# Layer norm of a graph attention block: variance, power and shift for two tiles in one instruction

## The chip, the cores and the metric

The kernel runs on one core of a Trainium2 chip. The metric is the time of one execution on the device in microseconds; lower is better. TensorE is called PE in the profile (its weight loads PEld), VectorE DVE, ScalarE ACT, GpSimd POOL and SyncE SP.

## The reference

The input `x` has 16 graphs of 1024 nodes with 512 features; `adj` is one 1024 x 1024 matrix of zeros and ones for all of them. The layer is multi-head attention over the neighbours of each node (8 heads of 64), an output projection, a residual and a layer norm without learned scale:

```python
q = (x @ Wq + bq).reshape(b, n, H, HD)
k = (x @ Wk + bk).reshape(b, n, H, HD)
v = (x @ Wv + bv).reshape(b, n, H, HD)
scores = jnp.einsum('bqhd,bkhd->bhqk', q, k) / jnp.sqrt(jnp.float32(HD))
scores = scores + (1.0 - adj)[None, None, :, :] * -1000000000.0
attn = jax.nn.softmax(scores, axis=-1)
out = jnp.einsum('bhqk,bkhd->bqhd', attn, v).reshape(b, n, d) @ Wo + bo
y = x + out
return (y - mean(y)) / jnp.sqrt(var(y) + 1e-5)
```

Each node has few neighbours, most of them 1 to 8, a few up to 80 in the kernel's tables.

## The kernel before

Nodes are sorted by their number of neighbours and put into tiles of 128 rows. For a tile, POOL gathers one neighbour's key and value rows per block (tile `kvg`, L1292); VectorE multiplies keys with queries (L1313) and sums per head (L1317), ACT takes the exponentials (L1328) and mostly also weighs the values (L1341), VectorE adds the blocks up (L1357) and divides by the sum of weights (L1387, tile `o`).

One Python loop writes the instructions of all engines in order. It counts block steps, `n` from -39 on; 530 steps are blocks. In each step it issues the exponentials of block n + 3, the products of block n + 4, gathers 8 blocks ahead, the sums, and then what earlier steps have planned: `later(k, fn)` puts `fn` into step n + k, in the middle of the step (list `plan`), and `later_last(k, fn)` puts it at the end of that step, behind ACT's weighting (list `rest`). Every engine works through its own instructions in this order and waits only for data and buffers.

Between these, a step gives PE a number of units, by a credit per step: those of `fronts`, which project x to queries, keys and values of the batches to come (L799 `pq`, L956), and those of `finish`, which multiply a finished tile by Wo (L799 `po`). The list `fronts` lasts until some 45 steps before the last block; the profile's last 165 us or so are that last stretch. There the tiles that had been spilled to memory come back (tile `oTs`).

The layer norm of a tile is written out by `complete` (L1097), one step behind its last matmul. VectorE adds the projected tile to the residual `y` and takes the row sums with it (L1112, L1113; `st[:, 0]`). One step later ACT squares the deviations and sums them (`spread`, L1120; `st[:, 2]`). `variance` (L1123, VectorE) scales that and adds epsilon; `power` (L1126, POOL) takes the power -1/2 (`st[:, 3]`); `shift` (L1129, VectorE) makes minus the mean times that (`st[:, 4]`); `norm_out` (L1134, ACT) applies both to `y`; `store` (L1148, POOL) scatters the rows to the output. VectorE's three are on one column of 128 rows each.

A tile is "single" while `fronts` isn't empty, if it has fewer than 128 rows, and at the very end. A single tile in front of the last stretch has its variance at step +3, its power at +4, its shift at +6 and its normalisation at the end of +7, its store at +9. In the last stretch, tiles of 128 rows go in pairs: the two share a statistics tile of two times five columns, the first waits in `half` for the second, each takes its own variance and its own shift, and POOL takes both powers in one instruction (L1174).

A tile `y` is loaded ahead of its `finish` (`load_y`, L1035 from SP or L1038 from POOL), into one of six buffers, while fewer than five are held; `del Y[b, t]` in `store` gives it back. The `finish` of a tile begins two steps behind its load at the earliest.

Of the kernel before, what the change touches and what calls it, by code (L numbers as in the profile page):

```python
# [14 lines left out]
OP = mybir.AluOpType  # L15
# [3 lines left out]
EPS = 1e-5  # L19
# [55 lines left out]
P = 128  # L75
# [103 lines left out]
def kernel(  # L179
# [36 lines left out]
    nc = tc.nc  # L216
    B, N, D = x.shape
# [37 lines left out]
    with ExitStack() as main:  # L255
# [192 lines left out]
        def later(k, fn):  # L448
            plan.setdefault(now[0] + k, []).append(fn)

        def later_last(k, fn):
            rest.setdefault(now[0] + k, []).append(fn)
# [554 lines left out]
        loaded, half, wide = {}, [], []  # L1007
# [7 lines left out]
        def rows_of(b, t):  # L1015

            if t == LONE_TILE or t == 0 and merged(b):
                n, col, base = (2 * SPARED, NT + 2, b - 1) if t else (P, NT + 1, b - 1)
            elif t == MORE_TILE:
                n, col, base = (LONE - SPARED) * (B - PAIRED_FROM), NT + 3, 0  # L1020
            else:
                n, col, base = P, NT if t == ONE_KEY and b >= PAIRED_FROM else t, b
            return n, asked_row[0:n, col:col + 1], base * N * D
# [19 lines left out]
        def load_lone(b):  # L1043


            Y[b, "mean"] = work.tile([P, D], F32, tag="y", name=f"means_{b}", bufs=Y_BUFS)
            for i in range(2):
                nc.sync.dma_start(
                    Y[b, "mean"][SPARED * i:SPARED * (i + 1), :], mean_rows[b - 1 + i:b + i, :].to_broadcast([SPARED, D])
                )  # L1050
            load_y(b, LONE_TILE)
            later(4, lambda: complete(b, LONE_TILE, Y.pop((b, "mean")), True))
# [15 lines left out]
        def finish(b, t):  # L1068


            mean_row = t == ONE_KEY and b >= PAIRED_FROM
            plain = bool(fronts) or mean_row
            biased = not plain and now[0] < total and number(b, t) in (*SPILL, -1)

            if not plain and not biased and (b, t) != closes[total - 1]:
                nc.vector.tensor_tensor(Y[b, t], Y[b, t], bo_bc, op=OP.add)

            def out(p):
                OT.pop((b, t))
                if mean_row:  # L1080
                    keep_mean(b, p)
                if not fronts and total - 4 < now[0] < total:
                    later(total - now[0], lambda: complete(b, t, p, plain))
                else:
                    complete(b, t, p, plain)

            units = product(f"po_{b}_{t}", lambda c: OT[b, t][:, ts(c, P)], W["o"], out)
            if biased:
                def bias():
                    nc.tensor.matmul(  # L1090
                        PS[f"po_{b}_{t}"], three.to_broadcast([P, P]), bo_3, start=False, stop=False
                    )

                units.insert(2, (BIAS, bias, None))
            return units

        def complete(b, t, p, plain):  # L1097
            n, rows, offset = rows_of(b, t)
            y, p = Y[b, t][0:n, :], p[0:n, :]
            ending = not fronts and now[0] >= total - 1  # L1100
            single = fronts or ending or n < P
            if single:
                st = small.tile([P, 5], F32, name="stats", bufs=6)[0:n, :]
            else:

                second = bool(half)
                if not second:
                    half.append([small.tile([P, 2, 5], F32, name="stats_2", bufs=5)])
                st2 = half[0][0]
                st = st2[:, int(second), :]  # L1110
            if plain:
                nc.vector.tensor_tensor(y, p, y, op=OP.add)  # L1112
            nc.vector.scalar_tensor_tensor(  # L1113
                y, bo_bc[0:n, :] if plain else p, 1.0, y, op0=OP.mult, op1=OP.add, accum_out=st[:, 0:1]
            )

            def spread():

                sq = work.tile([P, D], F32, tag="ysq", name=f"ysq_{b}_{t}", bufs=1)
                nc.scalar.activation(sq[0:n, :], y, AF.Square, bias=st[:, 0:1], scale=-float(D), accum_out=st[:, 2:3])  # L1120

            def variance():
                nc.vector.tensor_scalar(st[:, 2:3], st[:, 2:3], 1.0 / D ** 3, EPS, op0=OP.mult, op1=OP.add)  # L1123

            def power():
                nc.gpsimd.tensor_tensor(st[:, 3:4], st[:, 2:3], neg_half[0:n, :], op=OP.pow)  # L1126

            def shift():
                nc.vector.scalar_tensor_tensor(  # L1129
                    st[:, 4:5], st[:, 0:1], -1.0 / D, st[:, 3:4], op0=OP.mult, op1=OP.mult  # L1130
                )

            def norm_out():
                nc.scalar.activation(y, y, AF.Identity, bias=st[:, 4:5], scale=st[:, 3:4])  # L1134
                if not fronts and now[0] >= total:
                    later_last(1, store)
                else:
                    later(2, store)

            def centre():  # L1140
                nc.vector.tensor_scalar(st[:, 4:5], st[:, 0:1], 1.0 / D, None, op0=OP.mult)

            def last_norm_out():
                nc.vector.tensor_scalar(y, y, st[:, 4:5], st[:, 3:4], op0=OP.subtract, op1=OP.mult)
                store()

            def store():
                nc.gpsimd.indirect_dma_start(  # L1148
                    out=out_rows[b, t], out_offset=bass.IndirectOffsetOnAxis(ap=rows, axis=0),
                    in_=y, in_offset=None, element_offset=offset,  # L1150
                )
                del Y[b, t]

            later_last(0 if ending else 1, spread)
            if ending and (b, t) == closes[total - 1]:
                for step in (centre, variance, power, last_norm_out):
                    later(1, step)
            elif ending:
                later(1, variance)
                later(1, power)  # L1160
                later_last(1, shift)
                later_last(1, norm_out)
            elif single:
                late = 1 if fronts else 0
                later(2 + late, variance)
                later(3 + late, power)
                later(4 + 2 * late, shift)
                later_last(5 + 2 * late, norm_out)
            elif second:
                later(3, variance)  # L1170
                mate_shift, mate_norm_out = half.pop()[1]

                def powers():
                    nc.gpsimd.tensor_tensor(  # L1174
                        st2[:, :, 3:4], st2[:, :, 2:3], neg_half[:, :, None].to_broadcast([P, 2, 1]), op=OP.pow
                    )

                def shifts():
                    mate_shift()
                    shift()  # L1180

                later(4, powers)
                shift_at = 6 if fronts else min(6, max(5, total - now[0]))
                later(shift_at, shifts)
                later_last(shift_at, mate_norm_out)
                later_last(7 if shift_at == 6 else 5, norm_out)
            else:
                later(3, variance)
                mine = half[0]
                mine.append((shift, norm_out))  # L1190

                def alone():
                    if half and half[0] is mine:
                        half.pop()
                        power()
                        later(2, shift)
                        later_last(3, norm_out)

                later(6, alone)

# [281 lines left out]
        done, coming, spilled, gathered, fronts, guarded = [], [], [], [0], [], []  # L1484
# [31 lines left out]
        with tc.manual_schedule():  # L1516
# [20 lines left out]
            n = -LEAD_IN  # L1537
# [120 lines left out]
```

## Time and profile before

| | |
|---|---|
| runs | 1845.62, 1847.8, 1847.21 us |
| median | 1847.21 us |
| span of the profiled execution (its whole time is not given) | 1840.4 us |
| mean granted clock of PE over the span | 0.996 |
| DMA, mean | 303 GB/s |

The profile is of one execution. Its page lists the busy time of each engine, the span in 40 slices, and the costliest groups of instructions; further views give the waits, the instructions in order of time and the busy time by stretch. Some rows of the page's slices and groups, for orientation:

```profile
PE   7999999999999999999999999999999999999997
...
DVE  6889889999989999999999999999999999997986
ACT  3637869989889898999889988989799999987886
POOL 1367766766565776767757666677666767665786
PEclk9999999999999999999999999999999999999998
...
L1341 ACT ACTIVATE pv<-kvg,pv 128x64 f32<-128x64 f32 x3600 | 907.5, 341 | 0.0
L1292 POOL DMA_INDIRECT kvg<-kv_pair,place_row x462 | 526.7, 1140 | 307.4 <-ACT pv L1341 99.6
...
L1134 ACT ACTIVATE y<-y,stats 128x512 f32<-128x512 f32 (+1 forms) x128 | 102.7, 806 | 17.0 <-DVE stats L1129 17.0
```

A digit is the busy share of one slice of 46 us in tenths. In a group's row stand the line, engine, operation, output and inputs with their shapes and the count; then the busy time, the mean of one in ns, and the idle time of the engine just before, with what ended most of it.

### The profile page before, as it was taken

What the parts mean: (1) busy time and instruction counts of PE and PEld (TensorE: products, weight loads), DVE (VectorE), ACT (ScalarE), POOL (GpSimd) and SP (SyncE); (2) the same over time, 40 slices, a digit from 0 to 9 for tenths busy, and PEclk for the clock granted to TensorE, in tenths of its full rate; (3) what the DMA queues carried; (4) which work ended last, traced back from release to release, by engine and by line L of the source; (5) the groups of instructions that cost most, each with busy time, mean ns of one, the idle gap of its engine ahead of it and who ended that gap; (6) DMA issues with size and microseconds to landing.
All of it is one profiled execution on the core that took longest, in us unless ns stands there. A gap on an engine that the chain in (4) does not pass through costs nothing.

```text
span 1840.4 us, 25352 instructions
## 1 busy us (share of the span) xinstructions
PE 1798.2 (98%) x5140; PEld 876.2 (48%) x5140; DVE 1693.7 (92%) x3473; ACT 1563.2 (85%) x6183; POOL 1215.3 (66%) x1142
## 2 busy tenths in 40 slices
PE   7999999999999999999999999999999999999997
PEld 3444454554444454444444445444544444444443
DVE  6889889999989999999999999999999999997986
ACT  3637869989889898999889988989799999987886
POOL 1367766766565776767757666677666767665786
PEclk9999999999999999999999999999999999999998
DMA  7358787989889899999988998999989999889995
GB/s 287 106 190 253 256 325 237 346 301 327 308 280 314 295 336 319 344 316 308 347 316 310 346 335 276 343 321 322 339 315 325 314 355 326 306 324 325 338 319 191
DMA packets 198791, 558.54 MB, mean 303 GB/s; under 512 B 33450, under 2 KB 33470, under 8 KB 198626
## 3 DMA queue, kind: packets, MB, share of 16 engines
q0 software_dynamic: 112640, 370.50, 59.3%
q1 hardware_dynamic: 82910, 180.52, 26.2%
q10 hardware_dynamic: 3076, 5.82, 0.9%
q14 instruction: 122, 1.00, 0.2%
q8 instruction: 43, 0.70, 0.2%
HBM read 420.30 MB, written 157.45 MB: 314 GB/s over the span
## 4 chain that ended last, share of the span: by engine, by line
PE 69%; DVE 10%; ACT 9%; DMA 4%; issue 3%; POOL 1%; SPq 0%; POOLq 0%; DVEq 0%; ACTq 0%
PE po L799 17%; PE pq L799 15%; PE pp L956 12%; PE z L956 9%; PE x L956 9%; ACT pv L1341 5%; DVE qk L1313 2%; PE poT L1401 2%; PE pxT L757 2%; PE sum L1367 2%; DVE s L1317 2%; PE sum L1366 2%; DVE pv L1357 1%; ACT sq_k L809 1%; DMA kvg<-kv_pair,place_row 1%
## 5 line engine op out<-in xcount | busy, mean ns | idle before, releaser
L1341 ACT ACTIVATE pv<-kvg,pv 128x64 f32<-128x64 f32 x3600 | 907.5, 341 | 0.0
L1292 POOL DMA_INDIRECT kvg<-kv_pair,place_row x462 | 526.7, 1140 | 307.4 <-ACT pv L1341 99.6
L799 PE MATMUL pq<-wq,xT 128*128 128x512 f32 x792 | 367.8, 596 | 0.0
L1317 DVE TENSOR_REDUCE s<-qk 128x8 f32<-128x512 f32 x530 | 360.7, 681 | 6.8
L799 PE MATMUL po<-wo,oT 128*128 128x512 f32 x792 | 359.3, 594 | 0.7 <-ACT oT L1405 0.7
L1313 DVE TENSOR_TENSOR qk<-qt,kvg 128x512 f32<-128x512 f32 x434 | 297.2, 685 | 1.1 <-DMA kvg<-kv_rows,key_row 0.6
L956 PE MATMUL x<-b,xT 128*128 128x512 f32 x504 | 237.3, 593 | 0.5 <-ACT e L969 0.4
L956 PE MATMUL pp<-t,s 128*128 128x512 f32 x504 | 237.0, 593 | 0.0
L1357 DVE TENSOR_TENSOR pv<-pv,pv 128x520 f32<-128x520 f32 x329 | 228.3, 694 | 4.3 <-ACT pv L1341 4.2
L799 PEld LDWEIGHTS po<-wo,oT 128*128 128x128 f32 x792 | 149.1, 191 | 170.0 <-issue 160.2
L799 PEld LDWEIGHTS pq<-wq,xT 128*128 128x128 f32 x792 | 148.4, 192 | 161.9 <-issue 149.9
L1010 POOL DMA_INDIRECT x<-in_x_dram,asked_row x120 | 133.0, 1108 | 77.8 <-issue 21.3
L1148 POOL DMA_INDIRECT out_dram<-y,asked_row x129 | 146.9, 1139 | 39.1 <-issue 21.2
L1328 ACT ACTIVATE pv<-s,absent 128x8 f32<-128x8 f32 x434 | 127.0, 294 | 44.0 <-DVE s L1317 40.8
L809 ACT ACTIVATE sq_k<-kv 128x128 bf16<-128x128 f32 x512 | 150.8, 301 | 6.4 <-DVE kv L979 3.4
L956 PEld LDWEIGHTS pp<-t,s 128*128 128x128 f32 x504 | 94.7, 191 | 108.1 <-issue 99.4
L956 PEld LDWEIGHTS x<-b,xT 128*128 128x128 f32 x504 | 94.2, 191 | 107.4 <-issue 99.0
L956 PE MATMUL z<-b,s 128*128 128x512 f32 x252 | 119.2, 596 | 7.0 <-DVE kv L984 7.0
L1246 POOL DMA_INDIRECT qg<-q_rows,query_row x96 | 104.4, 1088 | 28.4 <-issue 26.9
L956 PE MATMUL z<-t,s 128*128 128x512 f32 x252 | 118.6, 593 | 0.0
L956 PE MATMUL pp<-t,xT 128*128 128x512 f32 x252 | 118.5, 593 | 0.0
L1134 ACT ACTIVATE y<-y,stats 128x512 f32<-128x512 f32 (+1 forms) x128 | 102.7, 806 | 17.0 <-DVE stats L1129 17.0
(279 smaller groups left out, 2713.0 us busy)
## 6 DMA issues: line engine op xcount, KB each, us to landing
kv_pair<-kv SPq DMA_DIRECT2D x98, 512.0 KB
q_rows<-q SPq DMA_DIRECT2D x106, 256.0 KB
qt<-q_rows SPq DMA_DIRECT2D x98, 256.0 KB
residual<-x SPq DMA_DIRECT2D x83, 256.0 KB
y<-residual SPq DMA_DIRECT2D x83, 256.0 KB
kv_rows<-kv SPq DMA_DIRECT2D x15, 512.0 KB
kvg<-kv_pair,place_row POOLq DMA_INDIRECT x462, 6.9
kv_pair<-kv SPq DMA_DIRECT2D x28, 256.0 KB
```

The costliest lines, as they stand in the source:

```text
L799: nc.tensor.matmul(p, lhs(c), w[:, c, :], start=(c == 0), stop=(c == NPAIR - 1))
L809: nc.scalar.activation(sq, s[:, ts(h, P)], AF.Square, scale=scale, accum_out=sums[:, h:h + 1])
L956: nc.tensor.matmul(R[bank], l[:, ts(c, P)], right[:, c, :], start=(first and c == 0), stop=(c == 1), skip_group_check=True,)
L1010: nc.gpsimd.indirect_dma_start(out=y, out_offset=None, in_=x_rows, in_offset=bass.IndirectOffsetOnAxis(ap=asked_row[:, t:t + 1], axis=0), ...
L1148: nc.gpsimd.indirect_dma_start(out=out_rows[b, t], out_offset=bass.IndirectOffsetOnAxis(ap=rows, axis=0), in_=y, in_offset=None, element_o ...
L1246: nc.gpsimd.indirect_dma_start(out=q, out_offset=None, in_=q_rows[b % ROWS], in_offset=bass.IndirectOffsetOnAxis(ap=rows, axis=0))
L1292: nc.gpsimd.indirect_dma_start(out=KG[n], out_offset=None, in_=rows, in_offset=bass.IndirectOffsetOnAxis(ap=(place_row if b else key_row)[ ...
L1313: nc.vector.tensor_tensor(QK[n], q, KG[n][:, 0:D], op=OP.mult)
L1317: nc.vector.tensor_reduce(S[n], QK.pop(n).rearrange("p (h d) -> p h d", d=HD), axis=AX.X, op=OP.add)
L1328: nc.scalar.activation(PV[n][:, D:], S.pop(n), AF.Exp, bias=bias)
L1341: nc.scalar.activation(pv[:, ts(h, HD)], v[:, ds(D + h * HD, HD)], AF.Copy, scale=pv[:, D + h:D + h + 1])
L1357: nc.vector.tensor_tensor(PV[b, t], PV[b, t], pv, op=OP.add)
```

## The change

A tile of 128 rows is now paired in the whole kernel, not only in the last stretch; single are tiles of fewer rows and those at the very end. Of a pair, the variance and the shift are one VectorE instruction over two columns each, as the power on POOL already was. The steps are counted from the second tile: variances +3, powers +4, shifts +6 (fewer near the end, as before), the first tile's normalisation at the end of the step of the shifts, the second's one step later. A first tile that gets no mate within 9 steps (5 in the last stretch, where it was 6) goes on alone: its variance in that step, power +1, shift +3, normalisation at the end of +4.

```diff
-            single = fronts or ending or n < P
+            single = ending or n < P
...
             elif second:
-                later(3, variance)
-                mate_shift, mate_norm_out = half.pop()[1]
+                mate_norm_out = half.pop()[1]
+
+                def variances():
+                    nc.vector.tensor_scalar(
+                        st2[:, :, 2:3], st2[:, :, 2:3], 1.0 / D ** 3, EPS, op0=OP.mult, op1=OP.add
+                    )
 
                 def powers():
                     nc.gpsimd.tensor_tensor(
...
                 def shifts():
-                    mate_shift()
-                    shift()
-
+                    nc.vector.scalar_tensor_tensor(
+                        st2[:, :, 4:5], st2[:, :, 0:1], -1.0 / D, st2[:, :, 3:4], op0=OP.mult, op1=OP.mult
+                    )
+
+                later(3, variances)
                 later(4, powers)
                 shift_at = 6 if fronts else min(6, max(5, total - now[0]))
                 later(shift_at, shifts)
                 later_last(shift_at, mate_norm_out)
                 later_last(7 if shift_at == 6 else 5, norm_out)
             else:
-                later(3, variance)
                 mine = half[0]
-                mine.append((shift, norm_out))
+                mine.append(norm_out)
 
                 def alone():
                     if half and half[0] is mine:
                         half.pop()
-                        power()
-                        later(2, shift)
-                        later_last(3, norm_out)
-
-                later(6, alone)
+                        variance()
+                        later(1, power)
+                        later(3, shift)
+                        later_last(4, norm_out)
+
+                later(9 if fronts else 5, alone)
```

## The prediction

> **What bounds the kernel now.** I read the page first (shares of busy time), then the busy time by stretch, then what TensorE waits for.
>
> ```profile
> span 1840.4 us, 25352 instructions
> ...
> PE 1798.2 (98%) x5140; PEld 876.2 (48%) x5140; DVE 1693.7 (92%) x3473; ACT 1563.2 (85%) x6183; POOL 1215.3 (66%) x1142
> ...
> 200.00:1650.00 1450.00, 1436.76 (x4156) 706.20 (x4155) 1378.11 (x2700) 1301.16 (x5300) 982.09 (x903) 1.00 0.91 317
> 1650.00:1790.00 140.00, 138.95 (x381) 65.49 (x380) 119.89 (x299) 111.76 (x385) 101.64 (x93) 1.00 0.92 327
> 1790.00:1841.00 51.00, 36.66 (x93) 16.78 (x92) 32.20 (x100) 35.13 (x103) 31.39 (x33) 0.88 0.55 202
> ```
>
> The last three rows give, for a stretch, its length and the busy time of PE, PEld, DVE, ACT and POOL, then the granted clock. From 200 to 1650 us, where pairing is new, PE is idle 1450 - 1436.8 = 13.2 us; in the next 140 us, 1.1 us. A busy PE need not be one at its peak, so I look at how fast the matmuls follow one another.
>
> ```profile
> 1000.02 1.88 PE L956 MATMUL pp<-t,s 128*128 128x512 f32 x4
> ...
> 1001.74 3.60 PE L799 MATMUL pq<-wq,xT 128*128 128x512 f32 x8
> ...
> 1005.17 1.88 PE L956 MATMUL x<-b,xT 128*128 128x512 f32 x4
> ```
>
> Four matmuls start in 1.72 us and eight in 3.43: one per 0.43 us, while the records last 0.59, so each runs into the next and nothing stands between them. The granted clock is 1.00. PE is therefore the bound from 200 to 1790 us, and a change that gives PE nothing less to do can win at most its 14.3 us of idle time there and something at the end.
>
> ```profile
> PE z L956 <- DVE kv L984: 5.9, 4, 3.0
> ...
> PE pm L867 <- DVE vsum L863: 3.1, 3, 1.9
> ...
> PE poT L1401 <- DVE o L1387: 2.6, 1, 2.6
> ...
> PE pq L799 <- DVE y L1112: 0.8, 1, 0.8
> ```
>
> These are PE's waits from 200 to 1650 us (total, times, longest): 12.4 us, all on VectorE. VectorE is the neighbour that matters, and the change takes instructions off it.
>
> **The change: VectorE.** A tile's layer norm has a variance (L1123), a power on POOL (L1126, or L1174 for two), a shift (L1129) and the normalisation on ACT (L1134).
>
> ```profile
> L1123 DVE TENSOR_SCALAR stats<-stats x129: 131/145/155, 195.7 to 1832.2; 128x1 f32<-128x1 f32 x121, 112x1 f32<-112x1 f32 x8
> ...
> L1129 DVE SCALAR_TENSOR_TENSOR stats<-stats x128: 137/151/202, 209.0 to 1830.4; 128x1 f32<-128x1 f32 x120, 112x1 f32<-112x1 f32 x8
> ...
> L1126 POOL TENSOR_TENSOR stats<-stats,neg_half x97: 543/585/1852, 205.6 to 1832.9; 128x1 f32<-128x1 f32 x89, 112x1 f32<-112x1 f32 x8
> L1174 POOL TENSOR_TENSOR stats<-stats,neg_half x16: 717/794/1761, 1699.5 to 1815.7; 128x2 f32<-128x2 f32 x16
> ...
> 1714.72 0.15 DVE L1378 TENSOR_TENSOR rden<-sum,pv 128x8 f32<-128x8 f32 x1
> 1714.79 0.68 DVE L1379 TENSOR_TENSOR o<-sum,pv 128x512 f32<-128x512 f32 x1
> ...
> 1718.91 0.22 DVE L1129 SCALAR_TENSOR_TENSOR stats<-stats 128x1 f32<-128x1 f32 x2
> 1719.05 0.15 DVE L1123 TENSOR_SCALAR stats<-stats 128x1 f32<-128x1 f32 x1
> 1719.11 0.69 DVE L1113 SCALAR_TENSOR_TENSOR y<-po,y 128x512 f32<-128x512 f32 x1
> ```
>
> A small record lasts 145 or 151 ns, but what it costs VectorE is when the next one starts: two shifts take 0.14 us (1718.91 to 1719.05), a variance 0.06. I take 67 and 62 ns. An instruction over two columns isn't in the trace on VectorE; one over eight (L1378) lets the next start after 0.07 us, one over one column after 0.06 to 0.07, so two columns cost no more than one.
>
> How many pairs? The order of VectorE's records tells the block step of each sum L1113: count the products L1313 ahead of it. While x is still being projected, full tiles come 2 to 12 steps apart. A first tile waits up to 9 steps for its mate. Going through the steps gives 38 pairs (from steps 11 and 15 to steps 475 and 480) and 8 tiles that stay alone; then the 16 pairs of L1174 as now. Removed on VectorE: 38 x (62 + 67) ns = 4.9 us in the first stretch, 16 x 129 ns = 2.1 us in the last.
>
> Little of that reaches PE, because VectorE catches up whenever it has to wait itself. The two longest waits of PE for z show it:
>
> ```profile
> 544.95 0.43 DVE L783 TENSOR_TENSOR s<-xT 128x256 f32<-128x256 f32 x1 [2.96 <-PE z L956]
> ...
> 549.82 1.98 PE L956 MATMUL z<-b,s 128*128 128x512 f32 x4 [2.38 <-DVE kv L984]
> ...
> 1063.61 0.43 DVE L783 TENSOR_TENSOR s<-xT 128x256 f32<-128x256 f32 x1 [0.35 <-ACT xT L761]
> ...
> 1065.88 1.98 PE L956 MATMUL z<-b,s 128*128 128x512 f32 x4 [3.01 <-DVE kv L984]
> ```
>
> In brackets stands the idle time before. VectorE was idle itself until 544.95 and 1063.61, and between that and the end of PE's wait it runs no variance and no shift. These 5.4 us stay. In the unbroken runs before the other waits I count 18 small instructions in all; with 0.4 of them gone, 18 x 0.4 x 0.065 = 0.5 us. Bounds: 0, and the whole 4.9.
>
> In the last stretch the power is paired already. There the one long wait of PE is
>
> ```profile
> 1808.33 1.02 PE L1401 MATMUL poT<-ident,o 128*128 128x128 f32 x4 [3.09 <-DVE stats L1123]
> ```
>
> The transpose needs o (L1387), which VectorE makes after a run of 15.6 us without a gap, with 8 small instructions in it; four go: 4 x 0.065 = 0.3 us. Bounds: 0 and 2.1.
>
> **The change: POOL.** 38 times two powers become one: 38 x (2 x 585 - 794) ns = 14 us. POOL also issues the gathers behind the power, but VectorE's wait for a gathered block is small:
>
> ```profile
> DVE qk L1313 <- DMA kvg<-kv_pair,place_row: 1.3, 2, 0.8
> ```
>
> I take 0, at best -1.3 us.
>
> **The change: ACT, the wait that is added.** A single tile has its shift at step +6 and its normalisation at the end of step +7. In a pair the first tile's normalisation stands at the end of the very step of the shift. Behind it in ACT's queue are the next exponentials, the weighting and the copies of e, xT and oT that PE waits for. In the last stretch this is so now:
>
> ```profile
> ACT y L1134 <- DVE stats L1129: 10.0, 6, 3.5
> ...
> ACT y L1134 <- DVE stats L1129: 7.0, 6, 1.5
> ...
> ACT e L969 <- PE x L956: 58.2, 29, 5.1
> ...
> PE po L799 <- ACT oT L1405: 0.3, 1, 0.3
> ```
>
> The first row is of 1650 to 1790 us, the second of the end: 17.0 us over 16 pairs. Nothing of the kind is listed from 200 to 1650 us, where all tiles are single. For each of the 38 steps I compared when the mate's shift ends with when ACT is through its weighting of that step. At the median ACT comes 1.5 us after the shift and would not wait; in 8 of 38 it comes earlier, by 8.3 us in total. The worst place:
>
> ```profile
> 268.32 0.71 ACT L1120 ACTIVATE ysq<-y,stats 128x512 f32<-128x512 f32 x1
> ...
> 270.20 0.15 DVE L1129 SCALAR_TENSOR_TENSOR stats<-stats 128x1 f32<-128x1 f32 x1
> ...
> 270.32 0.30 ACT L1328 ACTIVATE pv<-s,absent 128x8 f32<-128x8 f32 x1 [1.20 <-DVE s L1317]
> ```
>
> Here ACT would be held from about 268.4 to 270.4. Since ACT has slack towards PE (it waits 58.2 us for PE's x alone, PE for ACT 0.3 us, the last two rows of the fence before), I take +0.2 us; bounds 0 and 8.3.
>
> **The change: tiles held longer.** A first tile is stored up to 7 steps later. At most four loaded tiles are let stand beside a new one. By the steps this delays a load once, near step 485, where the projections end, by one step. If PE misses a product there it loses 4 x 0.43 = 1.7 us; the products behind find free steps, so I take 0. A load into a buffer not yet stored costs SP, not PE, as far as the trace shows (before 1650 us and after it):
>
> ```profile
> SPq L1035 <- DMA out_dram<-y,asked_row: 1.4, 1, 1.4
> ...
> SPq L1035 <- DMA out_dram<-y,asked_row: 36.1, 7, 15.5
> ```
>
> **The sum.** -0.5 - 0.3 + 0 + 0.2 + 0 = -0.6 us: a span of 1839.8 us. What lies around that execution's span is not given; the three runs shown are 5.2 to 7.4 us above it, their median, 1847.21, by 6.8. With 6.8 around it I forecast 1846.6.
>
> **Rivals.**
>
> *VectorE is the bound after all.* Then the 4.9 + 2.1 = 7.0 us come off whole: 1847.2 - 7.0 = 1840.2. For it: 1378 of 1450 us busy, and every wait of PE above is for VectorE. Against it: the matmuls without gaps and only 13.2 us of idle PE, 5.4 of them in places without a small instruction. A milder form, in which shorter runs on VectorE dissolve some waits of 2 to 3 us each, ends at about the same time. 0.22. The Trainium skill, "Perfetto Trace Analysis", section "Identifying the Most-Contended Engine", says that a matmul's busy share is no measure of the room left and that the weight loads' share is one. By that rule the 48% of PEld would leave PE half free and make VectorE the engine to relieve, as in this rival; the pitch of 0.43 us speaks against it here.
>
> *ACT waits for the shift.* The mechanism of the last section but two: the first tile's normalisation stops ACT's queue until VectorE reaches the shift, at the 8 places counted, and it goes through to PE in full: 1847.2 + 8.3 = 1855.5. It decides as soon as ACT runs ahead of VectorE in the step of the shift, as it does in the last stretch. Against it: ACT comes 1.5 us late at the median. 0.13.
>
> *It does not pair.* If mates mostly missed each other, nothing would change: 1847.2. The gaps of 2 to 12 steps speak against it. 0.03. *The delayed load costs a tile's turn at the end.* There the sums of successive tiles come 3.7 us apart:
>
> ```profile
> 1822.98 0.69 DVE L1113 SCALAR_TENSOR_TENSOR y<-po,y 128x512 f32<-128x512 f32 x1
> ...
> 1826.73 0.68 DVE L1113 SCALAR_TENSOR_TENSOR y<-po,y 128x512 f32<-128x512 f32 x1
> ```
>
> This would give 1847.2 - 0.8 + 3.7 + 1.7 = 1851.8. 0.05.
>
> By a page the saving of the first part would be larger: the Trainium skill, "VectorE: DVE Perf Modes", section "The TRN2 errata — SBUF-src ops pay a fixed extra latency per instruction", states a measured fixed term of about 150 cycles, 156 ns at its 0.96 GHz, so 108 instructions would save 17 us of VectorE. The pitch of 62 to 67 ns in this trace is less than half of that, and the sum above goes by the pitch.
>
> **How the numbers follow.** Forecast 0.57, the rivals 0.22, 0.13, 0.03, 0.05. A measurement of this kernel can tell about 0.2%, 3.7 us, from no change. The forecast's own range is 1843.5 to 1850: PE's waits of 2 to 3 us fall differently whenever instructions shift. The range goes down to the first rival and stops short of the second: 1839.5 to 1852. Faster: 0.22 + 0.03 of the forecast's low end = 0.25. Slower: 0.13 + 0.05 = 0.18. Within: 0.57.
>
> **What would show it.** Right: about 54 rows of two columns on each of L1123's successor, L1174 and the shift; PE's idle time from 200 to 1650 us still 10 to 16 us, its waits still on kv, vsum and o; a wait of ACT's L1134 for the shift now listed in that stretch, under 10 us. Wrong: idle time of PE there under 7 us (first rival), or over 20 with waits on ACT's copies (second); a hole in PE near 1680 us or a longer end (the last one).

## The result, and the profile after

| | before | after |
|---|---|---|
| median | 1847.21 us (1844.56 to 1849.67, 5 runs) | 1857.11 us (1852.9 to 1857.58, 5 runs) |
| span of the profiled execution | 1840.4 us | 1853.3 us |
| mean granted clock | 0.996 | 0.992 |

The ratio is 1.0045, with a 95% interval of 1.0033 to 1.0057: the change makes the kernel about 8 us slower by the ratio, 9.9 us by these medians. The forecast was 1846.6 us and the range ended at 1852. The two spans lie 12.9 us apart, more than the medians: a span is 1.8 us below the time of its own execution (in one of the runs below 1868.5 us beside 1870.28), so the profiled execution of the kernel before took about 1842 us, less than any of its five runs, and some 3 of the 12.9 us are the choice of execution.

The page of the changed kernel: busy time, share and instructions of each engine.

```profile
PE 1801.7 (97%) x5140; PEld 875.8 (47%) x5140; DVE 1687.6 (91%) x3365; ACT 1563.6 (84%) x6183; POOL 1200.4 (65%) x1104
```

VectorE has 3473 - 3365 = 108 instructions fewer and POOL 1142 - 1104 = 38 fewer, which is what the change should remove. Its groups by line show the pairs: name, count, then shortest, median and longest in ns, and the times of the first and the last.

```profile
L1173 DVE TENSOR_SCALAR stats<-stats x54: 152/161/418, 213.5 to 1825.3; 128x2 f32<-128x2 f32 x54
L1178 POOL TENSOR_TENSOR stats<-stats,neg_half x54: 714/750/1761, 220.8 to 1826.1; 128x2 f32<-128x2 f32 x54
L1183 DVE SCALAR_TENSOR_TENSOR stats<-stats x54: 141/153/197, 228.2 to 1828.9; 128x2 f32<-128x2 f32 x54
```

So it pairs, and VectorE and POOL are relieved. Busy time by stretch, changed kernel (length, then PE, PEld, DVE, ACT, POOL, granted clock):

```profile
200.00:1650.00 1450.00, 1437.25 (x4154) 704.88 (x4153) 1372.62 (x2625) 1300.45 (x5298) 965.72 (x865) 1.00 0.90 317
1650.00:1790.00 140.00, 135.75 (x370) 63.85 (x369) 115.17 (x266) 108.76 (x373) 95.78 (x88) 0.99 0.90 321
```

Where the pairing is new, PE is idle for 1450 - 1437.3 = 12.7 us, against 13.2; in the next 140 us it is idle for 4.2 us, against 1.1. The waits from 200 to 1650 us (total, times, longest) are the old ones and one more of ACT:

```profile
ACT y L1134 <- DVE stats L1183: 8.0, 7, 2.0
...
PE z L956 <- DVE kv L984: 6.5, 5, 2.9
...
PE pm L867 <- DVE vsum L863: 2.6, 3, 2.0
PE poT L1407 <- DVE o L1393: 2.5, 1, 2.5
```

The loss is all behind 1650 us, where the power had been paired before. PE in order of time, changed kernel (start, duration, line and tiles; in brackets the idle time before and its end):

```profile
1706.09 3.41 PE L799 MATMUL po<-wo,oTs 128*128 128x512 f32 x4 [3.34 <-DMA oTs<-spill]
...
1816.00 1.12 PE L1407 MATMUL poT<-ident,o 128*128 128x128 f32 x4 [8.93 <-DVE o L1393]
1816.90 3.62 PE L799 MATMUL po<-wo,oTs 128*128 128x512 f32 x4
1820.32 0.63 PE L1090 MATMUL po<-bo,three 128*128 128x512 bf16 x1
```

PE waits 3.3 us at 1706, for a spilled sum that is loaded late, and at 1816 for `o` 8.93 us, where it had waited 3.09. From that transpose to the end of the span it is 1853.3 - 1816.0 = 37.3 us; before, 1840.4 - 1808.3 = 32.1. Behind the transpose stand six output products in place of five. One of them, which starts at 1823.79, takes 3.65 us until the next starts.

What makes `o` late? VectorE sits idle twice shortly before, each time for a power on POOL. The changed kernel:

```profile
1797.71 0.16 DVE L1183 SCALAR_TENSOR_TENSOR stats<-stats 128x2 f32<-128x2 f32 x1 [3.02 <-POOL stats L1178]
1800.87 0.16 DVE L1129 SCALAR_TENSOR_TENSOR stats<-stats 112x1 f32<-112x1 f32 x1 [3.00 <-POOL stats L1126]
```

and the kernel before, where the second of these waits has its counterpart and the first is missing:

```profile
1792.69 0.16 DVE L1129 SCALAR_TENSOR_TENSOR stats<-stats 112x1 f32<-112x1 f32 x1 [2.19 <-POOL stats L1126]
```

From 1800.87 us on VectorE has no gap of a microsecond until `o` at 1815.25. POOL's queue in order of time shows why the powers are late. The changed kernel:

```profile
1785.60 1.03 POOL L1148 DMA_INDIRECT out_dram<-y,asked_row  x1 [0.30 <-issue]
1789.85 0.94 POOL L1038 DMA_INDIRECT y<-in_x_dram,asked_row  x1 [3.22 <-DMA out_dram<-y,asked_row]
1791.09 1.85 POOL L1252 DMA_INDIRECT qg<-q_rows,query_row  x1 [0.30 <-issue]
1793.25 1.02 POOL L1298 DMA_INDIRECT kvg<-kv_pair,place_row  x1 [0.31 <-DMA y<-in_x_dram,asked_row]
1794.58 1.03 POOL L1148 DMA_INDIRECT out_dram<-y,asked_row  x1 [0.30 <-issue]
1795.91 1.02 POOL L1298 DMA_INDIRECT kvg<-kv_pair,place_row  x1 [0.30 <-issue]
1796.95 0.73 POOL L1178 TENSOR_TENSOR stats<-stats,neg_half 128x2 f32<-128x2 f32 x1
...
1800.26 0.58 POOL L1126 TENSOR_TENSOR stats<-stats,neg_half 112x1 f32<-112x1 f32 x1
```

The load at 1789.85 stops POOL for 3.2 us, until a store gives its buffer `y` back. Behind it in the same queue stand gathers and stores, one every 1.3 us, and between them the powers that VectorE waits for. Before, the same load comes later by the step count and stops nothing:

```profile
1794.20 1.36 POOL L1038 DMA_INDIRECT y<-in_x_dram,asked_row  x1 [0.30 <-DVE y L1076]
```

Which load is it, and how does pairing two columns of statistics move it? Three rules of the kernel matter, which the loop applies in each step:

```python
for tile_done in done[...] + coming:
    if tile_done not in loaded and kept_y() < 5:
        load_y(*tile_done)
if lone_tiles and kept_y() < 4:
    load_lone(lone_tiles.pop(0))
...
if spilled and not fronts and n > last_reload + 1 and len(Y) - kept_y() < 7:
    reload(*spilled.pop(0), reloads)
```

`kept_y()` counts the loaded tiles in the six buffers that are not stored yet. `load_lone` loads a tile of 112 spared rows (56 of each of two graphs), with their means, and takes two of the buffers. `reload` brings a spilled sum back (`oTs` and its residual), at most every second step and while fewer than seven such tiles stand. Following these rules through the steps gives, for the tiles that move, the steps before and after:

| step of | before | after |
|---|---|---|
| store of (13,6), a first tile whose mate (14,2) comes five steps later | 484 | 488 |
| load, finish of (14,5): five tiles are held at step 485 | 485, 487 | 486, 488 |
| load of (14,1) | 487 | 488 |
| store of (4,3) | 498 | 499 |
| reload of (7,3): seven reloaded tiles stand at step 498 | 498 | 499 |
| every reload after it, to the last | 500, ... 528 | 501, ... 529 |
| finish of (8,3); of (15,2) and (15,1), which go ahead of it | 504; 505, 506 | 506; 504, 505 |
| store of (15,1) | 516 | 515 |
| load of the spared rows (15,8): three tiles are held | 518 | 515 |
| last finish ahead of the two steps, 528 and 529, that allow none | (15,7) | (12,6) |
| finishes from step 530 on | 3 | 4 |

This table is worked out from the kernel's order of instructions and has no times. It suggests two harms from one delayed store: the load of (15,8) comes three steps early, into a buffer that isn't free, and one output product slips behind the last blocks. The experiments separate them.

### The profile page after: what moved, and what is told of

Same layout as the page of the kernel before. It is cut to its first block, busy times and chain, and to the rows that moved or that the text cites. A ratio compares the mean times of both kernels' runs of the same rounds, so it can differ in the third digit from the quotient of the medians.

```text
span 1853.3 us, 25158 instructions
## 1 busy us (share of the span) xinstructions
PE 1801.7 (97%) x5140; PEld 875.8 (47%) x5140; DVE 1687.6 (91%) x3365; ACT 1563.6 (84%) x6183; POOL 1200.4 (65%) x1104
## 4 chain that ended last, share of the span: by engine, by line
PE 67%; DVE 9%; ACT 7%; DMA 7%; issue 4%; POOL 2%; SPq 0%; POOLq 0%; DVEq 0%; ACTq 0%
PE po L799 15%; PE pq L799 14%; PE pp L956 12%; PE z L956 9%; PE x L956 9%; ACT pv L1347 4%; DMA kvg<-kv_pair,place_row 2%; PE pxT L757 2%; PE poT L1407 2%; DVE qk L1319 2%; PE sum L1373 2%; DVE s L1323 2%; PE sum L1372 2%; DMA residual<-x 1%; DMA oTs<-spill 1%
## 5 line engine op out<-in xcount | busy, mean ns | idle before, releaser
L1134 ACT ACTIVATE y<-y,stats 128x512 f32<-128x512 f32 (+1 forms) x128 | 102.6, 806 | 32.2 <-DVE stats L1183 25.1
```

## The experiments

Three theories: **the slip**, one tile held four steps too long shifts the reloads, with the harms above; **ACT's wait** for the shift, the new one, costs the time; **VectorE's saving** is worth something that another effect hides. Each ratio is to the kernel before, on the same chip, with its 95% interval.

### Two tiles left single (e1_two_single)

```diff
-            single = ending or n < P
+            single = ending or n < P or (b, t) in ((13, 6), (14, 2))
```

> The changed kernel, but the two last tiles ahead of the last stretch, (13, 6) and (14, 2), stay single as before, so that (13, 6) is stored 9 steps after its sum and not 13; all other pairs stay. Theory of the hold: the loss comes from this one tile's buffer being held over the end of the projections, so the time is that of before within 2 us (1845 to 1849), PE loses under 2 us between 1690 and 1730 us, and its last long wait for o is about 3 us, not 9. Rival, the wait of ACT for the shift in the first stretch (8 us in the trace): still there, so the time stays at 1855 to 1858.

Measured: 1846.92 us, ratio 0.9995 [0.9982, 1.0009]. With 53 of the 54 pairs the whole loss is gone. PE's wait for `o` is 2.62 us; it still misses a reloaded sum, for 3.03 us at 1721.61, where I had expected under 2 us. ACT's wait from 200 to 1650 us stays:

```profile
ACT y L1134 <- DVE stats L1183: 8.0, 6, 2.0
```

So ACT's wait falls as the cause: it is there and costs nothing that can be measured. VectorE's saving brings nothing that can be measured here either, with 106 instructions fewer; whether ACT's wait hides it is left to e5.

### The tile held, and nothing paired anew (e2_before_held)

The kernel before, with the normalisation of (13,6) four steps later:

```diff
-                later_last(5 + 2 * late, norm_out)
+                later_last(5 + 2 * late + 4 * ((b, t) == (13, 6)), norm_out)
```

> The kernel before, with one thing alone from the change: the normalisation of tile (13, 6), and so its store, comes 4 steps later. No pairing is added. Theory of the hold: the whole loss appears, 1854 to 1859, with PE's wait of about 3 us for a reloaded tile near 1705 us and one of 8 to 9 us for o near 1815 us. Rival, ACT's wait for the shift: there is none here, so 1845 to 1849.

Measured: 1858.6 us, ratio 1.0056 [1.0038, 1.0074]: the whole loss, without the change. PE misses a reloaded sum for 3.74 us at 1708.88, and its wait for `o` is as in the changed kernel:

```profile
1819.79 1.12 PE L1401 MATMUL poT<-ident,o 128*128 128x128 f32 x4 [9.56 <-DVE stats L1123]
```

### Room for one more reloaded tile (e3_one_more_reload)

The changed kernel with the list of reloaded tiles one longer:

```diff
-                if spilled and not fronts and n > last_reload + 1 and len(Y) - kept_y() < 7:
+                if spilled and not fronts and n > last_reload + 1 and len(Y) - kept_y() < 8:
```

> The changed kernel, with room for one more tile in the list of reloaded residuals (8 for 7), so that the reloads keep their every-second-step rhythm at step 498 and the steps from 497 on are those of before; the tile (13, 6) is still held and its buffer still awaited. If the slip of the reloads by one step is what costs at the end, PE's 9 us wait near 1815 shrinks to 3 and the time is 1849 to 1852, with the wait near 1705 us left. If the wait for the buffer costs all of it, 1855 to 1858. If ACT's wait does, 1855 to 1858 too.

Measured: 1848.25 us, ratio 1.0009 [0.9999, 1.0018], a little better than expected. From step 498 on the reloads and the finishes go as before. PE in order of time, this kernel:

```profile
1708.19 3.78 PE L799 MATMUL po<-wo,oTs 128*128 128x512 f32 x4 [4.51 <-DMA oTs<-spill]
...
1815.61 0.66 PE L1407 MATMUL poT<-ident,o 128*128 128x128 f32 x4 [2.62 <-DVE o L1393]
```

The wait near 1706 is there still, longer than in the changed kernel, and the loss is nearly gone; the wait for `o` is back at 2.6 us. That wait, which I had first blamed, is worth at most some 3 us, the interval's end, and probably under 2.

### Another buffer for the load that SyncE waits for (e4_other_buffer)

SyncE's waits in the changed kernel from 1650 us on (total, times, longest):

```profile
SPq L1035 <- DMA out_dram<-y,asked_row: 52.3, 6, 14.1
```

The longest is for the buffer of (13,6), and the reload that PE misses at 1706 is queued behind it. Here the changed kernel loads (14,5) into the buffer of a projection weight, which is free by then:

```diff
+                if (b, t) == (14, 5):
+                    Y[b, t] = work.tile([P, 2, D], F32, tag="b22", ..., bufs=1)[:, 0, :]
```

> The changed kernel, with tile (14, 5) loaded into a buffer that is free by then (one of the projection's weights) and not into the one that (13, 6) holds; the steps are those of the changed kernel. If SyncE's wait of 14 us for that buffer, with the reloads queued behind it, causes PE's wait near 1705 us, that one goes and the time is 1850 to 1854; if the slip of a step causes all, 1855 to 1858 with both waits as they are.

Measured: 1857.24 us, ratio 1.005 [1.0033, 1.0067]. PE's wait at 1706 is gone and nothing is won. That alone doesn't price it, since two other waits of PE, 1.90 and 2.41 us, stand now near 1786:

```profile
1788.08 3.78 PE L799 MATMUL po<-wo,oTs 128*128 128x512 f32 x4 [2.41 <-DMA oTs<-spill]
```

The steps are the same as after the change, and so is the long wait for `o`:

```profile
1818.81 1.12 PE L1409 MATMUL poT<-ident,o 128*128 128x128 f32 x4 [8.70 <-DVE o L1395]
```

### ACT's wait taken away (e5_no_act_wait)

The kernel of e1_two_single, in which the first tile is normalised a step later in the stretch with the projections:

```diff
-                later_last(shift_at, mate_norm_out)
+                later_last(shift_at + bool(fronts), mate_norm_out)
```

> The kernel of e1_two_single, with one more edit: in the stretch with the projections the normalisation of a pair's first tile is issued a step after the pair's shift, as the second tile's is, and no longer in the same step. It takes away ScalarE's wait for the shift (8.0 us over 6 waits in e1's trace up to 1650 us). The first tile is held for a step longer. Theory (the wait is hidden, the loss was the reloads' slip alone): no change against e1's 1846.9 us, 1845.5 to 1848.5, with the wait gone from the trace. Rival (the saving on VectorE is there, and ScalarE's wait eats it): 1840 to 1844 us.

This run and the next two were on another chip, where the kernel before took 1873.7 us, so only the ratios can be compared. Measured: 1877.28 us, ratio 1.0023 [1.0005, 1.0042]. The wait of L1134 for L1183 is no longer listed before 1650 us, and the kernel isn't faster: no saving of VectorE comes out when ACT's wait goes. It may even be a little slower than e1_two_single, whose interval it just touches; whether that is the longer hold or the chip stays open.

### The slip alone (e6_slip_alone)

The kernel before, with one reload put off by a step:

```diff
-                if spilled and not fronts and n > last_reload + 1 and len(Y) - kept_y() < 7:
+                if spilled and not fronts and n > last_reload + 1 and n != 498 and len(Y) - kept_y() < 7:
```

> The kernel before, with nothing paired anew and no tile held longer; only the reload of a finished sum that is due at step 498 is put off to step 499, so that the reloads behind it, one every second step, come a step late to the end. Theory (the slip of this rhythm is the cause, by which one of the last output products moves from before the last two steps to behind them): 1854 to 1858 us, with a wait of 8 to 10 us of TensorE for o near 1816 us, and three products finished late turned into four. Rival (the step without an output product at 487, or the buffer that SyncE waits for near 1700 us, is part of the loss): under 1851 us, and a wait for o of at most 5 us.

Measured: 1879.9 us against 1873.7, ratio 1.0033 [1.0013, 1.0053]: most or all of the loss, from the slip at step 498 alone. PE's wait for `o` is the long one (total, times, longest, from 1650 us on), and POOL stops at the load of (15,8):

```profile
PE poT L1401 <- DVE stats L1123: 10.3, 1, 10.3
```

```profile
1819.97 2.46 POOL L1038 DMA_INDIRECT y<-in_x_dram,asked_row  x1 [3.86 <-DMA out_dram<-y,asked_row]
```

### The reloads ahead of their rhythm (e7_reload_ahead)

The kernel of e1_two_single, reloading on consecutive steps twice, so that only two products are left behind the last blocks:

```diff
-                if spilled and not fronts and n > last_reload + 1 and len(Y) - kept_y() < 7:
+                if spilled and not fronts and n > last_reload + (n not in (499, 506)) and len(Y) - kept_y() < 9:
```

> The kernel of e1_two_single with the reloads of the last stretch brought ahead by a step twice (a reload on consecutive steps at 499 and 506, and nine tiles allowed in place of seven), so that two output products in place of three are left for behind the last two steps. A product is 16 matmuls of 0.43 us, 6.9 us. If each product left for the end costs the time that it takes there: 1838 to 1842 us. If TensorE has no idle time left ahead of the last steps other than the 3 us waits (its busy time was 40.00 of 40.00 us from 1750 to 1790 in e1), so that a product moved ahead only pushes the rest back: 1844 to 1848 us. I expect the second; over 1850 us would mean that the products at the end cover a wait.

Measured: 1889.15 us, ratio 1.008 [1.0052, 1.0108]. By the ratio that is 1862 us where the kernel before takes 1847: neither of the first two cases but the third, far beyond its bound. The size of a product was wrong too. The kernel reloads 23 sums, and in the changed kernel 184 matmuls read them:

```profile
L799 PE MATMUL po<-wo,oTs x184: 592/592/1221, 1686.9 to 1837.9; 128*128 128x512 f32 x184
```

So a product is 8 matmuls, 3.4 us, half of what I had expected. I had thought of products alone; the trace of e7 shows POOL and VectorE waiting in turn:

```profile
1825.96 0.96 POOL L1038 DMA_INDIRECT y<-in_x_dram,asked_row  x1 [2.45 <-DMA out_dram<-y,asked_row]
```

```profile
1836.17 0.16 DVE L1129 SCALAR_TENSOR_TENSOR stats<-stats 112x1 f32<-112x1 f32 x1 [8.32 <-POOL stats L1126]
```

PE waits 7.71 us for `o` here. This miss sent me from PE's queue to POOL's, and to the load of (15,8), which the traces with a long wait for `o` up to here had in common. By the steps it comes at 515 in all of them (the changed kernel, e2, e4, e6, e7), and POOL stops there for 2.45 to 3.86 us; in the kernel before, e1, e3 and e5 it comes at 518, and POOL's wait is 0.30 us.

### The two harms apart (e8 to e11)

Four kernels on one chip. The changed kernel with (15,8) loaded at step 518 again, while the reloads stay late and four products stay at the end:

```diff
-                if lone_tiles and kept_y() < 4:
+                if lone_tiles and kept_y() < 4 and n not in (515, 516, 517):
```

> The changed kernel with the late reloads left as they are and one thing put back: the load of the last tile of spared rows (15,8), which the late reloads brought from step 518 to step 515, may not come before 518. Four output products still stand behind the last two steps in place of three. Theory L (this load is the harm: in the changed kernel's trace GpSimd waits 3.22 us at 1789.85 us for a store to give it a y buffer, the gathers and powers queued behind it come late, VectorE waits 3.02 and 3.00 us for two of the powers, and so o is late and TensorE waits 8.9 us): no such waits, TensorE's wait for o back to 2.5 to 4 us, ratio 0.999 to 1.002. Theory P (the product that slipped behind the end is the harm): the wait for o stays at 8 us or more, ratio 1.004 to 1.006. A ratio of 1.002 to 1.004 with a short wait would mean both.

The kernel before with (15,8) loaded at step 515, three products at the end:

```diff
-                if lone_tiles and kept_y() < 4:
+                if lone_tiles and kept_y() < 4 + (n == 515):
```

> The kernel before with nothing paired anew, no tile held and the reloads in their old rhythm; only the load of the last tile of spared rows (15,8) is let through at step 515 in place of 518. Three products stay behind the last two steps. Theory L: GpSimd waits 2.5 to 4 us for a store at this load, TensorE 7 to 10 us for o, ratio 1.003 to 1.006. Theory P: no change, 0.999 to 1.001, with a wait for o of about 3 us.

The kernel of e1_two_single with (15,8) loaded at step 521:

```diff
-                if lone_tiles and kept_y() < 4:
+                if lone_tiles and kept_y() < 4 and n not in (518, 519, 520):
```

> The kernel of e1_two_single with the load of (15,8) put off the other way, from step 518 to 521. If the 2.6 to 3 us that TensorE waits for o in every kernel that loads it at 518 come from this tile too (before: VectorE waits 2.19 us for a power at 1792.69 us, ahead of o), the wait falls under 1.5 us and the ratio is 0.998 to 0.999; if that wait has another cause: 0.999 to 1.001, nothing that can be told from no change. If the tile then ends the kernel, over 1.002.

And the changed kernel without an edit:

> The changed kernel again, unedited, on the chip that the three others run on, as their measure: 1.0045 as before, 1.0033 to 1.0057, with TensorE's wait for o of 8 to 10 us and GpSimd's wait of 3 to 4 us at the load of (15,8).

| | reloads, products at the end | (15,8) loaded at | median, us | ratio |
|---|---|---|---|---|
| before | in time, 3 | 518 | 1847.52 | |
| e11, the changed kernel | late, 4 | 515 | 1856.5 | 1.0054 [1.0039, 1.0068] |
| e8 | late, 4 | 518 | 1851.16 | 1.0021 [1.0011, 1.003] |
| e9 | in time, 3 | 515 | 1853.58 | 1.0034 [1.0022, 1.0046] |
| e10 | in time, 3 | 521 | 1847.45 | 1.0005 [0.9993, 1.0017] |

Both harms are real. Without the early load 0.0021 is left (e8), and the early load adds 0.0054 - 0.0021 = 0.0033 to it (e11). e9 has nearly the same, 0.0034, for the early load alone, but that the two agree is luck in part: in e9 four tiles are held when the load takes its two buffers, so all six are taken, and in the changed kernel three. The 0.0021 isn't the late product alone either: e8 also misses a reloaded sum for 2.33 us at 1706.35, as e3 does, whose ratio is 1.0009. In e8 one of VectorE's two waits for POOL is gone, and PE waits 4.75 us:

```profile
1797.18 0.16 DVE L1129 SCALAR_TENSOR_TENSOR stats<-stats 112x1 f32<-112x1 f32 x1 [2.26 <-POOL stats L1126]
```

```profile
1812.04 1.11 PE L1407 MATMUL poT<-ident,o 128*128 128x128 f32 x4 [4.75 <-DVE o L1393]
```

In e11 beside it that transpose comes at 1817.00 us:

```profile
1817.00 1.11 PE L1407 MATMUL poT<-ident,o 128*128 128x128 f32 x4 [8.93 <-DVE o L1393]
```

So without the early load `o` is there 5.0 us sooner, and the median is 5.3 us lower. What is left in e8 lies mostly behind that transpose: with four products it is 1849.0 - 1812.0 = 37.0 us to the end of e8's span and 1853.5 - 1817.0 = 36.5 in e11; with three, 1847.7 - 1815.6 = 32.1 in e3 and 34.2 in e10, whose transpose is at

```profile
1811.40 0.66 PE L1407 MATMUL poT<-ident,o 128*128 128x128 f32 x4 [1.42 <-DVE o L1393]
```

in a span of 1845.6. The difference, 2 to 5 us, is about one product of 8 matmuls, 3.4 us.

e9 came out by the time of theory L, but not by its place. POOL stops longer than I expected, and SyncE, which has to find buffers for the loads behind, stands for most of 20 us; PE misses a reloaded sum and not `o`. POOL, SyncE and PE in this kernel:

```profile
1795.82 1.45 POOL L1038 DMA_INDIRECT y<-in_x_dram,asked_row  x1 [4.58 <-DMA out_dram<-y,asked_row]
```

```profile
1784.71 20.13 SPq L1035 DMA_DIRECT2D y<-residual  x2
```

```profile
1809.18 3.78 PE L799 MATMUL po<-wo,oTs 128*128 128x512 f32 x4 [6.29 <-DMA oTs<-spill]
```

VectorE's two waits for powers are there too, 4.88 and 2.96 us, but PE, held up by the missing sum, doesn't wait for `o` after them. Thus in e9 the early load does its harm through the buffers that it takes; how much of the harm in the changed kernel comes that way and how much through POOL's queue was not tried. e10 shortens the wait for `o` to 1.42 us and wins nothing that can be told from no change. A short wait of VectorE for POOL ahead of `o` does not set PE's wait by itself: it is 2.11 us in e10, and in e1, where PE waits 2.62 us, it is 0.76. In e11 POOL stops for 2.88 us at the early load, a little less than expected. None of these versions beats the kernel before.

## Why the prediction was wrong

- **What bounds the kernel.** Right for the stretch with the projections: PE idles 12.7 us there instead of 13.2, with the same three waits. For the end I looked at VectorE's run before `o` and counted its small instructions, but not at what starts that run: a wait for POOL, 2.19 us before the change, and two of 3.02 and 3.00 us after it.
- **VectorE.** 38 + 16 pairs and 108 instructions fewer, as counted; two columns cost nearly what one costs (median 153 ns against 151 for the shift, 161 against 145 for the variance). Its busy time fell by 1693.7 - 1687.6 = 6.1 us, near the 7.0 by the pitch. The Trainium skill, "VectorE: DVE Perf Modes", section "The TRN2 errata — SBUF-src ops pay a fixed extra latency per instruction", gives by its fixed term an estimate of 17 us. The trace does not bear that out for such short instructions: 6.1 us. That about nothing of it reaches PE was right: 0.9995 with 53 pairs.
- **POOL.** 14 us predicted, 1215.3 - 1200.4 = 14.9 measured. "I take 0" held for the powers that were saved. That POOL's order sets the end did not occur to me.
- **ACT.** 8.3 us over 8 waits predicted, 8.0 over 7 measured, cost taken at 0.2 us; e1_two_single keeps the wait and loses nothing. The rival built on it, with 0.13, falls.
- **"Tiles held longer": the step that failed.** The prediction says that "by the steps this delays a load once, near step 485", and "the products behind find free steps, so I take 0". The first half is nearly right: (14,5), 485 to 486, and (14,1) behind it. The second is wrong. The products do find free steps, by 495, but the stores behind them are a step late, (4,3) at 499, and the reloads have no free steps: they go every second step, their list is full at 498, and the step lost there is never made up. The term that I took as 0 is the whole loss: 1.0056 when the tile alone is held (e2), 1.0033 when the reload alone slips (e6).
- **The rival on that step.** "The delayed load costs a tile's turn at the end" named the right place and the right sign, at 1851.8 us and with a chance of 0.05. Its signs came too, a missed sum near 1706 us and a longer end. Its price was one turn of 3.7 us and one missed product of 1.7 us, which is half a product. What is left without the early load is about that, 0.0021 or 3.9 us (e8). What was missing is a second consequence of about 6 us (0.0033, e11 against e8): an order changed by one step lets the tile of spared rows through the gate of `kept_y() < 4` three steps early.
- **What lies around the span.** The sum adds 6.8 us for it. The runs show 1.8; the other 5 is that the profiled execution of the kernel before was quicker than its median. The forecast doesn't suffer, since it is that median less 0.6.
- **VectorE as the bound**, 0.22, falls with e1. The Trainium skill, "Perfetto Trace Analysis", section "Identifying the Most-Contended Engine", judges the room left on PE by its share of the peak rate, which isn't worked out here, and by the weight loads' share. The 48% of PEld would make VectorE the engine to relieve; relieved by 106 instructions, the kernel's time didn't move (0.9995).

## What to carry to other kernels

Where a loop hands out buffers and turns by thresholds, holding one tile longer isn't priced by the one load that it delays: follow each threshold behind it to the last step, since a rhythm with no slack keeps a lost step to the end, and a changed order can open another gate too early. An engine that is busy 65% of the time can set the end, as here, when one instruction in its queue waits for a buffer and other engines' small inputs stand behind it. When a wait moves, ask of the engine waited for what it had been waiting for itself: here it took three such steps, from PE over VectorE to POOL, to find the load.

## What the runs showed of the hardware beyond that

After some pauses PE is slower. After the 8.93 us without work the next four matmuls of the changed kernel, shown above, take 1820.32 - 1816.90 = 3.42 us, 0.85 us each, and the granted clock from 1816 to 1821 us is 0.50.

In the kernel before, a pause of 3.09 us does nearly the same, 1812.23 - 1809.14 = 3.09 us:

```profile
1809.14 3.25 PE L799 MATMUL po<-wo,oTs 128*128 128x512 f32 x4
1812.23 0.38 PE L1090 MATMUL po<-bo,three 128*128 128x512 bf16 x1
```

In e1_two_single a pause of 2.62 us does nothing, 1816.49 - 1814.77 = 1.72 us:

```profile
1814.28 0.66 PE L1407 MATMUL poT<-ident,o 128*128 128x128 f32 x4 [2.62 <-DVE o L1393]
1814.77 1.88 PE L799 MATMUL po<-wo,oTs 128*128 128x512 f32 x4
1816.49 0.38 PE L1090 MATMUL po<-bo,three 128*128 128x512 bf16 x1
```

In e3_one_more_reload a pause just as long, the 2.62 us before the transpose at 1815.61, does slow PE, 1819.34 - 1816.11 = 3.23 us:

```profile
1816.11 3.44 PE L799 MATMUL po<-wo,oTs 128*128 128x512 f32 x4
1819.34 0.56 PE L1090 MATMUL po<-bo,three 128*128 128x512 bf16 x1
```

The granted clock is 1.00 from 1814 to 1818 us in e1_two_single and 0.61 from 1815.6 to 1820 in e3_one_more_reload. So the length of the pause alone doesn't decide it; what else does stays open. Where PE slows in these kernels, it loses 1.4 to 1.7 us over four matmuls. That is a small part of the change's loss at most, since the kernel before has most of it too. The Trainium skill, "TensorE: Matmul & The Clock Gate", section "HAM oscillation — how this bites in real kernels", puts the limit at idle gaps of about 3.4 us and the clock behind them at half. The half agrees (0.85 against 0.43 us); the limit doesn't, since here 3.09 us and once 2.62 us were enough.

A buffer is free much later than its store is issued. In the changed kernel the last store ahead of the load at 1789.85 is issued at 1785.60, 4.25 us earlier, and the load still waits for a store; if it waits for an earlier one, the time is longer.
